# A graph-attention kernel on one core: another shape for the one-hot picks that replace part of the gathers

## The chip, the core and the metric

The kernel runs on one core of a Trainium2 chip. The metric is the device time of one execution in microseconds (us); three runs of the kernel before gave 4651.4 us as the median (4637.57 to 4661.18). The core's engines work side by side, each on its own queue of instructions in order: TensorE (PE, with its weight loads shown apart as PEld), VectorE (DVE), ScalarE (ACT), GpSimd (POOL) and SyncE (SP, which here only issues DMAs). They are tied together by semaphores.

## What is computed

Three layers of a graph transformer with 64 features, 6250 nodes and 206250 edges sorted by their target node, then a log-softmax, and a layer norm over the sum with the input. Cut to what matters here, one layer is

```python
q = x @ Wq + bq; k = x @ Wk + bk; v = x @ Wv + bv
e = edge_attr @ We
kj = k[src] + e
alpha = jnp.sum(q[dst] * kj, axis=-1) / jnp.sqrt(jnp.float32(D))
amax = jax.ops.segment_max(alpha, dst, num_segments=N)
p = jnp.exp(alpha - amax[dst])
denom = jax.ops.segment_sum(p, dst, num_segments=N)
w = p / denom[dst]
msg = (v[src] + e) * w[:, None]
agg = jax.ops.segment_sum(msg, dst, num_segments=N)
```

`x[src]` is the costly part: for each edge one row of 64 floats, from a place that the data decides, in every layer.

## The kernel before, in words

**Tiles.** Edges are cut into 403 chunks of 512 (`CH`), a chunk into four tiles (`T`) of 128. Four chunks (`LB`) make a batch, so a batch has 16 tiles and there are 101 batches. The program of all engines is written out in one order by Python generators (`tc.manual_schedule`): the main loop (L1660 to L1724) takes one batch as a "unit" u per round and interleaves sums of unit u-2 (`sums`, L1514), the transposed weights of u-1 (`weights`, L1506), the scores of u (`scores`, L1480), four turns of the next rows (`turn`, L1464), the ends of finished nodes (`finish`, L1309), and the picks for unit u+1.

**Rows by gather.** `gather` (L572) issues one indirect DMA from POOL for each tile of 128 edges (L578), which fetches 128 rows of x. `release` (L603) lets a chunk's gathers go when ACT has copied its indices to a `gate` tile (L609).

**Rows by pick.** In layer 0 the edges of each chunk are also sorted on the fly (`mark`, `Move`, `sorter`), so that tile t = 0 of each chunk has only source nodes of the first 18 blocks of 128 nodes (`RB`), and tile t = 3 only of the last 18. For some of those tiles no gather is issued; the rows are made on PE instead. `PICKS` says how many tiles of a batch: 3 in layer 0, 6 in layers 1 and 2, in the order of `spots` (t = 0 of chunks 0 to 3, then t = 3). `parts` holds the 36 blocks of x as a high and a low part. A source node in such a range has a block number 0 to 17, which is split into h, the group of `KB` = 4 blocks, and a place in the group; the key h*128 + (node mod 128) is compared with `rank` to give a one-hot.

The class `Picker` does this for two tiles (a pair) at a time:

- `aim` (L1169): two matmuls with the constant `coef` (L1182) spread the pair's keys over all partitions in PSUM (tag "m" in layers 1 and 2, "p" in layer 0); one DVE comparison (L1196) writes `NH` = 5 one-hots for both tiles, 128 x 1280 elements, to `hot`. Before the first pair of a batch, `which` (L1188) marks each edge's place in its group.
- `batch` (L1204): takes a pair, first aims the next one, then runs for each tile 5 groups x 2 parts = 10 matmuls (L1218; four groups of 256 columns and one of 128) into one half of a PSUM bank (tag "x", in layer 0 "s"); then DVE multiplies with `which` (L1229) and adds the four places in two steps (L1232, L1233), the last into the tile's place in the features.

`some` (L1652) advances the picks by a third of the batch's number of tiles at three places of a unit.

**Sorted order kept in DRAM.** `Move.drain` (L1010) writes a tile `to` with 32 rows for each chunk (five bits of the target's place, a row of ones, and the source node's numbers) to `toS` by one DMA of ACT's queue. Each later use loads it with one DMA of SP's (`decode`, L1604, three units ahead) into one of four `to` buffers. Both `aim` and `scores` read it; `scores` (L1484) multiplies it with `codeS`, 128 x 128. `Move.index` (L1033) computes the source indices in the new order and `kbs`, each edge's place in its group.

The picks' lines, and the order in which `aim` and the matmuls stand, are in the functions printed here:

Of the kernel before, what the change touches and what calls it, by code (L numbers as in the profile page):

```python
# [19 lines left out]
P = 128  # L20
D = 64
# [13 lines left out]
KB = 4  # L35
# [6 lines left out]
PICKS = ((3,), (6,), (6,))  # L42
LEAD = (4, 1, 1)


def slot(j):

    return j % 2 * (LB // 2) + j // 2
# [378 lines left out]
def main_path(  # L427
# [82 lines left out]
    tos = ctx.enter_context(tc.tile_pool(name="tos", bufs=4))  # L510
# [30 lines left out]
    toS = dram.tile([NT, P, CH], BF16, name="toS")  # L541
# [129 lines left out]
    def locate(k, m):  # L671

        half = CH // 2
        for i in range(2):
            at = slice(k * CH + i * half, k * CH + (i + 1) * half)
            room = picks.tile([P, NH, 2 * P], F32R, name="hot").rearrange("p h e -> p (h e)").bitcast(F32)
# [145 lines left out]
    codeS = const.tile([P, P], BF16, name="codeS")  # L822
    coef = const.tile([P, LB, P], BF16, name="coef")
    pickc = const.tile([P, 2, LB], BF16, name="pickc")
    kbs = const.tile([P, NT, 2, LB], BF16, name="kbs")
# [3 lines left out]
    def tools():  # L829
# [4 lines left out]
        room = picks.tile([P, 2, KB, D], F32, name="rows_of_b", bufs=1).rearrange("p s b d -> p (s b d)")  # L834
        two, wide = room[:, :LB], room[:, P : 2 * P]
        at = [ident[:, i::W] for i in range(ROW_K + 1)]
        nc.vector.scalar_tensor_tensor(two, at[ROW_H], float(P), at[ROW_P], ALU.mult, ALU.add)
        nc.vector.tensor_copy(coef, two.unsqueeze(2).to_broadcast([P, LB, P]))
        nc.vector.scalar_tensor_tensor(pickc[:, 0], at[ROW_B], float(P), at[ROW_P], ALU.mult, ALU.add)
        nc.vector.tensor_copy(pickc[:, 1], at[ROW_K])  # L840
        nc.vector.memset(wide, 0.0)
        for j in range(LB):
            rows = slice(slot(j) * W, (slot(j) + 1) * W)
            nc.vector.tensor_copy(wide[rows, j * W : j * W + BITS + 1], bit[rows, :])
        pc = ps("a")
        nc.tensor.transpose(pc[:, :P], wide, ident)
        nc.vector.tensor_scalar(codeS, pc[:, :P], FAR, None, ALU.mult)
# [6 lines left out]
    def mark(g):  # L854
# [56 lines left out]
        nc.vector.scalar_tensor_tensor(whole[1], lh[:, 1], -float(OFF), misc[:, ROW_B - 1], ALU.mult, ALU.add)  # L911
        yield
        nc.vector.tensor_scalar(whole[0], whole[1], KB.bit_length() - 1, None, ALU.logical_shift_right)
        nc.vector.tensor_copy(misc[:, ROW_H - 1], whole[0])
        nc.vector.tensor_scalar(whole[0], whole[1], KB - 1, None, ALU.bitwise_and)
        nc.vector.tensor_copy(misc[:, ROW_K - 1], whole[0])
# [24 lines left out]
    class Move:  # L941
# [68 lines left out]
        def drain(self):  # L1010
# [6 lines left out]
            nc.scalar.dma_start(toS[self.k], self.to)  # L1017
# [15 lines left out]
        def index(self):  # L1033

            k = self.k
            pi = ps("a")[:, : T * 2 * LB].rearrange("p (t v c) -> p t v c", t=T, v=2)
# [116 lines left out]
    class Picker:  # L1153


        def __init__(self, layer):
            self.layer = layer
            self.todo = []
            for k in range(len(batches)):
                those = spots(picked(layer, k))  # L1160
                for t in (0, T - 1):
                    cs = [c for c, i in those if i == t]
                    self.todo += [(k, t, cs[i : i + 2]) for i in range(0, len(cs), 2)]
            self.aimed = []
            self.which = {}
            self.side = 0
            self.keys = ps("m") if layer else None

        def aim(self):  # L1169

            if not self.todo or (self.layer, self.todo[0][0]) not in codes:
                return
            k, t, cs = self.todo.pop(0)
            n = len(cs)
            to = codes[self.layer, k]
            if self.layer:
                self.side = 1 - self.side
                pk = self.keys[:, self.side * 2 * P :][:, : n * P]
            else:
                pk = ps("p")[:, : n * P]  # L1180
            for s, c in enumerate(cs):
                nc.tensor.matmul(  # L1182
                    pk[:, s * P : (s + 1) * P], coef[:, c, :], to[:, t * P : (t + 1) * P], start=True, stop=True
                )
            if (self.layer, k) not in self.which:
# [9 lines left out]
            hot = picks.tile([P, NH, 2 * P], F32R, name="hot")[:, :, : n * P]  # L1195
            nc.vector.tensor_tensor(  # L1196
                hot,
                pk.unsqueeze(1).to_broadcast([P, NH, n * P]),
                rank.unsqueeze(2).to_broadcast([P, NH, n * P]),
                ALU.is_equal,  # L1200
            )
            self.aimed.append((k, t, cs, hot, self.which[self.layer, k]))

        def batch(self, k):  # L1204
# [3 lines left out]
            while self.aimed and self.aimed[0][0] == k:  # L1208
                _, t, cs, hot, which = self.aimed.pop(0)
                self.aim()  # L1210
                n = len(cs)
                px = ps("x" if self.layer else "s").rearrange("p (s b d) -> p s b d", s=2, b=KB)
                b0 = RB if t else 0
                for s in range(n):
                    for m, h in enumerate((0, *reversed(range(1, NH)))):
                        w = min(KB, RB - h * KB)
                        for i in range(2):
                            nc.tensor.matmul(  # L1218
                                px[:, s, :w].rearrange("p b d -> p (b d)"),
                                hot[:, h, s * P : (s + 1) * P],  # L1220
                                parts[:, i, b0 + h * KB : b0 + h * KB + w, :].rearrange("p b d -> p (b d)"),
                                start=(m == 0 and i == 0),
                                stop=(m == NH - 1 and i == 1),
                            )
                    if s + 1 < n:
                        yield
                at = (LB if t else 0) + cs[0]
                rows = picks.tile([P, 2, KB, D], F32, name="rows_of_b", bufs=1)[:, :n]
                nc.vector.tensor_tensor(  # L1229
                    rows, px[:, :n], which[:, at : at + n, :].unsqueeze(3).to_broadcast([P, n, KB, D]), ALU.mult  # L1230
                )
                nc.vector.tensor_tensor(rows[:, :, : KB // 2], rows[:, :, : KB // 2], rows[:, :, KB // 2 :], ALU.add)  # L1232
# [599 lines left out]
```

## Time and profile before

| what | value |
|---|---|
| median of three runs | 4651.4 us (4637.57 to 4661.18) |
| the profiled execution, its own time | 4656.6 us |
| its span, first to last instruction | 4654.9 us |
| mean granted TensorE clock | 0.966 |
| PE, PEld busy | 4216.7, 3111.6 us |
| DVE, ACT, POOL busy | 3829.2, 1995.7, 3337.9 us |
| gathers (POOL L578) | 3380 in all |
| pick matmuls (L1218) | 14560 |

The page divides the span into layer 0 (to about 1860 us, with the sorting), layer 1 (about 1980 to 3200 us) and layer 2 (about 3330 us to the end); between them PE's busy share falls for some 120 us. "Busy" is the union of an engine's instructions. In the group rows the numbers after the bar are busy us, mean ns of one, and the idle time of the engine just before, with what ended most of it; in the timeline the first column is the start in us from the span's start, the second the length of the merged run. A window view gives, for each engine, busy us and number of instructions.

### The profile page before, as it was taken

To read this page: it belongs to the slowest core of one execution; us is meant where nothing else is said; L and a number is where in the kernel's file an instruction comes from. 1 tells how busy PE (TensorE), PEld (TensorE's weight loads), DVE (VectorE), ACT (ScalarE), POOL (GpSimd) and SP (SyncE) were. 2 spreads that over 40 slices of the span, in tenths; PEclk is the share of its full clock that TensorE was granted. 3 is DMA by queue.
4 is the path that set the end of the run, shared out by engine and by line. 5 is a ranking of instruction groups with operands and counts; after the bars stand their busy time and mean duration, and the time that the engine had idled before them with its cause. 6 is when DMAs were issued, how large, how long until landed. Compare 5 with 4: busy or idle time off the path is not lost.

```text
span 4654.9 us, 117245 instructions
## 1 busy us (share of the span) xinstructions
PE 4216.7 (91%) x41145; PEld 3111.6 (67%) x41145; DVE 3829.2 (82%) x9064; ACT 1995.7 (43%) x5733; POOL 3337.9 (72%) x3390
## 2 busy tenths in 40 slices
PE   6889999999999999689999999999699999999996
PEld 3445555555555555367888888887478778878874
DVE  6778888898888888478888888888478888888885
ACT  2455555555555555333333333333234333334443
POOL 6777777777777766277777777777477777777774
PEclk9999999999999999799999999999799999999997
DMA  8787777777777777445555565555356655656553
GB/s 188 192 210 184 188 204 188 189 195 200 199 198 193 192 197 189 125 102 132 137 139 137 138 144 138 140 138 129 86 128 143 141 135 135 138 130 143 136 135 81
DMA packets 769749, 725.47 MB, mean 156 GB/s; under 512 B 403478, under 2 KB 544880, under 8 KB 769156
## 3 DMA queue, kind: packets, MB, share of 16 engines
q1 hardware_dynamic: 572564, 480.73, 43.5%
q0 software_dynamic: 108160, 110.97, 12.7%
q10 hardware_dynamic: 88432, 126.17, 7.7%
q8 instruction: 334, 5.47, 0.5%
q14 instruction: 259, 2.12, 0.2%
HBM read 557.62 MB, written 159.87 MB: 154 GB/s over the span
## 4 chain that ended last, share of the span: by engine, by line


## 5 line engine op out<-in xcount | busy, mean ns | idle before, releaser
L578 POOL DMA_INDIRECT feat<-x,gate x2004 | 1924.4, 960 | 613.9 <-issue 471.5
L578 POOL DMA_INDIRECT feat<-in_x,gate x1328 | 1365.8, 1028 | 526.2 <-issue 317.1
L1218 PE MATMUL ps_x<-parts,hot 128*128 128x256 f32 (+1 forms) x11880 | 1567.1, 288 | 0.0
L1218 PEld LDWEIGHTS ps_x<-parts,hot 128*128 128x128 f32 x11880 | 1457.1, 193 | 0.0
L1476 ACT COPY featT<-ps_a 64x256 f32<-64x256 f32 x2380 | 872.4, 367 | 1305.8 <-PE ps_a L1473 1265.2
L1196 DVE TENSOR_TENSOR hot<-ps_m,rank 128x1280 fp32r<-128x1280 f32 x594 | 879.9, 1481 | 33.1 <-PE ps_m L1182 32.9
L993 PE MATMUL ps_x<-hit,thirds 128*64 128x512 bf16 x4800 | 637.7, 393 | 5.5 <-DVE hit L983 5.1
L1473 PE MATMUL ps_a<-ident,feat 128*128 128x128 f32 x2380 | 488.0, 283 | 64.0 <-DMA feat<-x,gate 40.4
L983 DVE TENSOR_SCALAR hit<-ruler,pos 128x512 bf16<-128x512 f16 x1600 | 504.6, 363 | 1.7 <-PE ps_m L1002 1.5
L1473 PEld LDWEIGHTS ps_a<-ident,feat 128*128 128x128 f32 x2380 | 281.9, 140 | 333.4 <-issue 287.5
L1229 DVE TENSOR_TENSOR rows_of_b<-ps_x,which 128x512 f32<-128x512 f32 x594 | 406.4, 684 | 88.1 <-PE ps_x L1218 87.1
L1502 ACT ACTIVATE prob<-ps_s,part 128x512 f32<-128x512 f32 (+1 forms) x306 | 210.6, 688 | 625.6 <-DVE part L1500 500.0
L1218 PE MATMUL ps_s<-parts,hot 128*128 128x256 f32 (+1 forms) x2680 | 392.3, 294 | 30.9 <-ACT prob L1502 30.9
L993 PEld LDWEIGHTS <-thirds 128*64 128x64 bf16 x4800 | 233.2, 111 | 230.5 <-issue 83.6
L1218 PEld LDWEIGHTS ps_s<-parts,hot 128*128 128x128 f32 x2680 | 340.8, 195 | 60.7 <-ACT prob L1502 40.7
L1498 DVE TENSOR_REDUCE most<-ps_s 128x1 f32<-128x512 f32 (+1 forms) x306 | 211.2, 690 | 189.4 <-PE ps_s L1488 181.4
L1232 DVE TENSOR_TENSOR rows_of_b<-rows_of_b 128x256 f32<-128x256 f32 (+1 forms) x776 | 321.0, 414 | 26.6
L1522 PE MATMUL ps_g<-feat,probT 128*32 128x128 f32 x9672 | 338.2, 279 | 4.1 <-DVE y L1366 2.3
L1488 PE MATMUL ps_s<-featT,q 128*32 128x512 f32 x2418 | 336.3, 611 | 5.9 <-ACT featT L1469 5.2
L1522 PEld LDWEIGHTS ps_g<-feat,probT 128*32 128x32 f32 x9672 | 263.5, 111 | 52.6 <-issue 34.0
L1512 DVE COPY probT<-ps_p 128x512 f32<-128x512 f32 (+1 forms) x306 | 209.2, 684 | 99.0 <-PE ps_p L1510 97.3
L1182 PEld LDWEIGHTS <-coef 128*128 128x128 bf16 x1456 | 134.7, 99 | 190.5 <-issue 175.1
(226 smaller groups left out, 4392.6 us busy)
## 6 DMA issues: line engine op xcount, KB each, us to landing
feat<-eaP SPq DMA_DIRECT2D x296, 512.0 KB
featT<-eaS SPq DMA_DIRECT2D x296, 512.0 KB
raw<-in_ea SPq DMA_DIRECT2D x200, 256.0 KB
eaS<-eT ACTq DMA_DIRECT2D x200, 256.0 KB
eaP<-eN ACTq DMA_DIRECT2D x200, 256.0 KB
to<-toS SPq DMA_DIRECT2D x296, 128.0 KB
feat<-x,gate POOLq DMA_INDIRECT x2004
feat<-in_x,gate POOLq DMA_INDIRECT x1328
```

The costliest lines, as they stand in the source:

```text
L578: nc.gpsimd.indirect_dma_start(out=feat[:, c, t, 0], out_offset=None, in_=xts[layer][:, :], in_offset=bass.IndirectOffsetOnAxis(ap=index[: ...
L983: nc.vector.tensor_scalar(hit, ruler, self.pos[:, at : at + 1], None, ALU.is_equal)
L993: nc.tensor.matmul(self.px[i][j * D : (j + 1) * D, :], self.thirds[i][:, part, (j * T + t) * D : (j * T + t + 1) * D], self.hits[t, 2 * i ...
L1196: nc.vector.tensor_tensor(hot, pk.unsqueeze(1).to_broadcast([P, NH, n * P]), rank.unsqueeze(2).to_broadcast([P, NH, n * P]), ALU.is_equal,)
L1218: nc.tensor.matmul(px[:, s, :w].rearrange("p b d -> p (b d)"), hot[:, h, s * P : (s + 1) * P], parts[:, i, b0 + h * KB : b0 + h * KB + w, ...
L1229: nc.vector.tensor_tensor(rows, px[:, :n], which[:, at : at + n, :].unsqueeze(3).to_broadcast([P, n, KB, D]), ALU.mult)
L1232: nc.vector.tensor_tensor(rows[:, :, : KB // 2], rows[:, :, : KB // 2], rows[:, :, KB // 2 :], ALU.add)
L1473: nc.tensor.transpose(pt[:, t // 2 * P : (t // 2 + 1) * P], rows[:, t * D : (t + 2) * D], ident)
L1476: nc.scalar.copy(featT[:, :, h, :], pt[h * D : (h + 1) * D, : T // 2 * P].rearrange("d (i e) -> d i e", e=P))
L1488: nc.tensor.matmul(self.p_s[slot(j) * W : (slot(j) + 1) * W, :], self.q[:, j * STRIDE : j * STRIDE + W], self.featT[:, j, :], start=False, ...
L1498: nc.vector.tensor_reduce(top[:n], self.p_s[:n], AX.X, ALU.max)
L1522: nc.tensor.matmul(p_g[rows, :].rearrange("n (h d) -> n h d", h=2), self.probT[:, t, rows], batch[:, c + j, t], start=(t == 0), stop=(t == ...
```

## The change

Six blocks make a group instead of four (`KB` = 6), so 18 blocks need `NH` = 3 one-hots instead of 5, and a tile 6 matmuls of 384 columns each instead of 10. `PICKS` becomes 7, 6, 7 tiles in turn in layers 1 and 2 (6.67 on average); layer 0 stays at 3.

The keys are no longer spread by matmuls on each use. `Move.index` computes each batch's keys once (one matmul with `keyc`, one ACT copy) and stores them in DRAM as fp16 (`keyS`); `decode` loads a batch's keys to all partitions by one DMA, three units ahead, into one of three `keys` buffers. `aim` now takes all tiles of a batch with the same t at once (up to four), and makes its one-hots from `keys` in SBUF with `NH` DVE instructions, one for each group.

Each tile has a PSUM bank of its own: in layers 1 and 2 three in turn (two of tag "x" and "m"), in layer 0 "p" and "s" in turn. DVE multiplies for each tile, and one `tensor_reduce` for two tiles adds the six places.

`toS` keeps only the six rows of each chunk that `scores` needs; `drain` writes them with four DMAs. A unit loads its own 24 rows one unit ahead into one of two buffers, and `scores` always uses `codeT`. `mark` works out group and place with comparisons instead of shifts.

```diff
-KB = 4
+KB = 6
-PICKS = ((3,), (6,), (6,))
+PICKS = ((3,), (7, 6, 7), (7, 6, 7))
+MOST = max(n for p in PICKS for n in p)
...
-    tos = ctx.enter_context(tc.tile_pool(name="tos", bufs=4))
+    tos = ctx.enter_context(tc.tile_pool(name="tos", bufs=2))
...
-    toS = dram.tile([NT, P, CH], BF16, name="toS")
+    toS = dram.tile([NT, LB, BITS + 1, CH], BF16, name="toS")
+    keyS = dram.tile([NT, 2, LB, P], FP16, name="keyS")
...
-        nc.vector.tensor_scalar(whole[0], whole[1], KB.bit_length() - 1, None, ALU.logical_shift_right)
-        nc.vector.tensor_copy(misc[:, ROW_H - 1], whole[0])
-        nc.vector.tensor_scalar(whole[0], whole[1], KB - 1, None, ALU.bitwise_and)
-        nc.vector.tensor_copy(misc[:, ROW_K - 1], whole[0])
+        block, h = spare[:, 1], misc[:, ROW_H - 1]
+        nc.vector.scalar_tensor_tensor(block, lh[:, 1], -float(OFF), misc[:, ROW_B - 1], ALU.mult, ALU.add)
+        nc.vector.tensor_scalar(h, block, float(KB), None, ALU.is_ge)
+        for i in range(2, NH):
+            nc.vector.scalar_tensor_tensor(h, block, float(i * KB), h, ALU.is_ge, ALU.add)
+        nc.vector.scalar_tensor_tensor(misc[:, ROW_K - 1], h, -float(KB), block, ALU.mult, ALU.add)
...
-            nc.scalar.dma_start(toS[self.k], self.to)
+            for c in range(LB):
+                nc.scalar.dma_start(toS[self.k, c], self.to[c * W : c * W + BITS + 1])
...
+            pk = pa[:LB, 2 * P :].rearrange("c (t e) -> c t e", t=2)
+            nc.tensor.matmul(
+                pk, keyc, self.to.rearrange("r (t e) -> r t e", t=T)[:, :: T - 1], start=True, stop=True
+            )
+            key = small.tile([LB, 2, P], FP16, name="key", bufs=1)
+            nc.scalar.copy(key, pk)
+            nc.scalar.dma_start(keyS[k].rearrange("t c e -> c t e"), key)
...
-            for s, c in enumerate(cs):
-                nc.tensor.matmul(
-                    pk[:, s * P : (s + 1) * P], coef[:, c, :], to[:, t * P : (t + 1) * P], start=True, stop=True
-                )
...
-            hot = picks.tile([P, NH, 2 * P], F32R, name="hot")[:, :, : n * P]
-            nc.vector.tensor_tensor(
-                hot,
-                pk.unsqueeze(1).to_broadcast([P, NH, n * P]),
-                rank.unsqueeze(2).to_broadcast([P, NH, n * P]),
-                ALU.is_equal,
-            )
+            hot = picks.tile([P, NH, LB * P], F32R, name="hot", bufs=2)[:, :, : n * P]
+            for h in range(NH):
+                nc.vector.tensor_scalar(
+                    hot[:, h], keys[self.layer, k][:, first : first + n * P], rank[:, h : h + 1], None, ALU.is_equal
+                )
...
+                for s, c in enumerate(cs):
+                    px = ps(("xxm" if self.layer else "ps")[self.turn])[:, : KB * D].rearrange("p (b d) -> p b d", b=KB)
+                    self.turn = (self.turn + 1) % (3 if self.layer else 2)
+                    for h in range(NH):
...
+                    nc.vector.tensor_tensor(
+                        rows[:, s % 2], px, which[:, at].unsqueeze(2).to_broadcast([P, KB, D]), ALU.mult
+                    )
+                    if s % 2 or s + 1 == len(cs):
+                        n = s % 2 + 1
+                        nc.vector.tensor_reduce(
+                            loaded[self.layer, k][:, c - n + 1 : c + 1, t, 0],
+                            rows[:, :n].rearrange("p s b d -> p s d b"),
+                            AX.X,
+                            ALU.add,
+                        )
...
-            if self.placed:
-                self.to = codes[layer, self.k]
-                return
             self.to = tos.tile([P, CH], BF16, name="to")
+            here = toS[self.k] if self.placed else places[c : c + m]
+            nc.sync.dma_start(self.to[: m * (BITS + 1), :], here.rearrange("c b e -> (c b) e"))
...
-            codes[layer, k] = tos.tile([P, CH], BF16, name="to")
-            nc.sync.dma_start(codes[layer, k], toS[k])
+            keys[layer, k] = picks.tile([P, MOST * P], FP16, name="keys")
+            nc.sync.dma_start(
+                keys[layer, k][:, : n * P],
+                keyS[k].rearrange("t c e -> (t c e)")[: n * P].partition_broadcast(P),
+            )
```

76 lines of the change are left out of this document (21 added, 55 removed).

## The prediction

> **What bounds the kernel now.** I read the windows by stage first, then the groups of one stage, then the waits, then a timeline of one batch. One window inside layer 0 and one inside layer 1:
>
> ```profile
> core 0: us, PE busy (x) PEld busy (x) DVE busy (x) ACT busy (x) POOL busy (x), PEclk, DMA share, GB/s
> 500.00:1800.00 1300.00, 1217.86 (x12036) 744.35 (x12032) 1131.84 (x3401) 694.44 (x1771) 938.88 (x926) 0.99 0.77 194
> 2400.00:3200.00 800.00, 763.03 (x7718) 642.67 (x7710) 695.81 (x1277) 302.51 (x994) 607.19 (x633) 1.00 0.59 138
> ```
>
> By busy share PE bounds layer 1 (95%) and POOL (76%) has room. The groups of that window say otherwise:
>
> ```profile
> L578 POOL DMA_INDIRECT feat<-x,gate x633 | 607.8, 960 | 193.1 <-issue 145.5 <-DMA feat<-x,gate 25.6 <-ACT gate L609 9.4
> ...
> L1196 DVE TENSOR_TENSOR hot<-ps_m,rank 128x1280 fp32r<-128x1280 f32 x189 | 279.8, 1481 | 5.0 <-PE ps_m L1182 5.0
> ...
> L1229 DVE TENSOR_TENSOR rows_of_b<-ps_x,which 128x512 f32<-128x512 f32 x189 | 129.1, 683 | 16.9 <-PE ps_x L1218 16.9
> ...
> L1232 DVE TENSOR_TENSOR rows_of_b<-rows_of_b 128x256 f32<-128x256 f32 x190 | 81.3, 428 | 6.5
> ...
> L1233 DVE TENSOR_TENSOR feat<-rows_of_b 128x128 f32<-128x128 f32 x190 | 56.6, 298 | 6.8 <-DVE rows_of_b L1232 0.3
> ...
> L1498 DVE TENSOR_REDUCE most<-ps_s 128x1 f32<-128x512 f32 x63 | 43.5, 691 | 37.9 <-PE ps_s L1488 37.9
> ```
>
> 189 one-hot comparisons at 3 a batch are 63 batches in 800 us: 12.70 us a batch. POOL's row: 607.8 busy and 193.1 idle make 800.9, the whole window, and the idle time is 0.305 us ahead of each of 633 gathers. So gathers run back to back at 800/633 = 1.264 us, ten a batch (12.64 us): **POOL paces layers 1 and 2.** PE is close behind: 12.11 us busy a batch, and what it waits for is the one-hot:
>
> ```profile
> PE ps_m L1182 <- DVE hot L1196: 35.5, 32, 1.6
> ...
> PE ps_a L1473 <- DMA feat<-x,gate: 1.3, 3, 0.7
> ```
>
> DVE is busy 695.81/63 = 11.04 us. Three engines within 13% of each other: what comes after depends on all three, so I cost the change on each.
>
> **The change on POOL.** A mean of 6.67 picked tiles leaves 9.33 gathers: 9.33 x 1.264 = 11.80 us a batch, 0.90 less.
>
> **On PE.** One batch's picks in the timeline:
>
> ```profile
> 2507.47 0.68 DVE L1229 TENSOR_TENSOR rows_of_b<-ps_x,which 128x512 f32<-128x512 f32 x1
> 2507.61 0.27 PE L1182 MATMUL ps_m<-to,coef 128*128 128x128 bf16 x2 [0.88 <-DVE hot L1196]
> ...
> 2507.69 2.60 PE L1218 MATMUL ps_x<-parts,hot 128*128 128x256 f32 x20
> 2508.19 0.43 DVE L1232 TENSOR_TENSOR rows_of_b<-rows_of_b 128x256 f32<-128x256 f32 x1
> 2508.65 0.29 DVE L1233 TENSOR_TENSOR feat<-rows_of_b 128x128 f32<-128x128 f32 x1
> 2508.86 1.48 DVE L1196 TENSOR_TENSOR hot<-ps_m,rank 128x1280 fp32r<-128x1280 f32 x1
> ...
> 2510.24 0.25 PEld L1182 LDWEIGHTS <-coef 128*128 128x128 bf16 x2
> ...
> 2510.45 2.42 PEld L1218 LDWEIGHTS ps_x<-parts,hot 128*128 128x128 f32 x20
> ```
>
> A narrow view inside such a pair shows matmuls of 256 columns alone:
>
> ```profile
> 2508.47 0.76 PE L1218 MATMUL ps_x<-parts,hot 128*128 128x256 f32 x5
> ```
>
> Five starts, the last lasting 0.28: (0.76 - 0.28)/4 = 0.12 us from one to the next. A pair's 20 take (2.60 - 0.28)/19 x 20 = 2.44, so 1.22 a tile. A matmul of 384 columns isn't in the trace. If time goes by matmuls it costs 0.12 and a tile 6 x 0.12 = 0.72; if by columns 0.18 and a tile 1.08. I take the columns, the dearer: 6.67 x 1.08 = 7.20 against 6 x 1.22 = 7.32 (from below 4.80). The key matmuls go: their weight loads hold the path from 2510.24 to 2510.45, 0.21 us a pair, 0.63 a batch. The wait for the one-hot (35.5/63 = 0.56) should go too, since a group's one-hots are asked for a whole group of up to four tiles ahead instead of two. PE: 12.11 - 0.63 - 0.12 = 11.36 us. It no longer decides.
>
> **On DVE.** This is where the change pays. The prices of the new forms come from these rows (single lines' views, and groups over the whole span):
>
> ```profile
> L740 DVE TENSOR_SCALAR start<-start,low x4: 468/475/481, 18.6 to 141.4; 128x512 f32<-128x512 int32 x3, 19x512 f32<-19x512 int32 x1
> ...
> L1395 DVE TENSOR_SCALAR y<-y,lse x49: 242/247/444, 3568.7 to 4646.1; 128x64 f32<-128x64 f32 x49
> ...
> L1229 DVE TENSOR_TENSOR rows_of_b<-ps_s,which 128x256 f32<-128x256 f32 x96 | 39.3, 410 | 3.0 <-PE ps_s L1218 3.0
> ...
> L1389 DVE TENSOR_REDUCE lse<-ex 128x4 f32<-128x256 f32 x11 | 4.5, 410 | 0.0
> ...
> L983 DVE TENSOR_SCALAR hit<-ruler,pos 128x512 bf16<-128x512 f16 x1600 | 504.6, 363 | 1.7 <-PE ps_m L1002 1.5
> ```
>
> - One-hot, SBUF to SBUF, a scalar of each partition, four bytes out: L740 is nearest, 0.475 us at 512 elements; with L1395 (0.247 at 64) the slope gives 0.41 at 384 and 0.345 at 256. I add 0.03 for outliers like L1395's 444. Seven tiles: 3 x (0.51 + 0.44) = 2.85; six: 3 x (0.51 + 0.375) = 2.66; mean 2.79. From below 3 x 2 x 0.36 = 2.2 (the hit's price), from above the present comparison's 1.16 ns an element: 6.67 x 384 x 1.16 = 2.97.
> - Multiply from PSUM: between 0.410 (256) and 0.683 (512), 0.547 at 384; x 6.67 = 3.65.
> - `tensor_reduce` over two tiles, 768 elements read at a step of 64: 0.410 (256, L1389) and 0.691 (512) give 0.97; 0.55 for one tile. Seven: 3 x 0.97 + 0.55 = 3.46; six 2.91; mean 3.28. All rows of this operation read neighbours, so the stride's price is the unknown: below, 0.97; above, see the rivals.
>
> Added 9.72. Removed 3 x (1.481 + 0.683 + 0.428 + 0.298) = 8.67. Summed like this DVE goes to 11.04 + 1.05 = 12.1. But lengths overlap where nothing is awaited: the comparison at 2508.86 starts 0.08 us before L1233 ends (2508.94), while L1232 starts 0.04 after L1229 ends. Before, some two such joints a pair (0.4 a batch); after, about twelve (hot to hot, hot to multiply, multiply to multiply, reduce to the next) at 0.07: 0.8. So 11.04 + 1.05 - 0.4 = 11.7 busy, with small gaps of some 0.3 **about 12.0 us**; without any overlap gained, 12.5.
>
> Bank waits: a tile needs the bank of the tile three before, so PE can run three tiles (3.2 us) ahead of DVE; DVE's work between, the score maximum and a group's one-hots, is 0.69 + 1.4. I count nothing for it.
>
> **Together,** layers 1 and 2 go from 12.70 to the slowest of 11.80, 11.36 and 12.0, and I add 0.15 for engines that are so level: 12.15. Saved 0.55 x 99 batches x 2 = 109 us.
>
> The Trainium skill has a rule against this: "SBUF — State Buffer", "Who interferes with whom": a VectorE op in a two-port mode, which `tensor_scalar` in SBUF can enter, locks GpSimd out for the whole instruction. The one-hots move from a PSUM read to just that. This case's rows on it:
>
> ```profile
> L578 POOL DMA_INDIRECT feat<-x,gate x2004 | 1924.4, 960 | 613.9 <-issue 471.5 <-DMA feat<-x,gate 66.5 <-ACT gate L609 30.9
> ...
> L578 POOL DMA_INDIRECT feat<-in_x,gate x1328 | 1365.8, 1028 | 526.2 <-issue 317.1 <-ACT gate L609 122.9 <-DMA feat<-in_x,gate 14.6
> ```
>
> A gather takes 1028 in layer 0, where 1600 hits hold DVE 504.6 of 1860 us (27%), and 960 without them. If all 68 ns come from the hits, one-hots at 2.79/12.15 = 23% add 58: POOL 9.33 x 1.32 = 12.3, rival 2 below. If no gather went on during a one-hot, POOL would take 11.80 + 2.79 = 14.6, rival 5; by the rule taken whole that would be so, but then the hits' 27% would have stretched layer 0's gathers by more than 7%.
>
> **Layer 0.** The same groups in the window 500 to 1800:
>
> ```profile
> L578 POOL DMA_INDIRECT feat<-in_x,gate x926 | 940.0, 1015 | 361.4 <-issue 220.1 <-ACT gate L609 84.3 <-ACT mm L1329 10.1
> ...
> L1196 DVE TENSOR_TENSOR hot<-ps_p,rank 128x1280 fp32r<-128x1280 f32 x71 | 105.0, 1479 | 0.0
> ...
> L1196 DVE TENSOR_TENSOR hot<-ps_p,rank 128x640 fp32r<-128x640 f32 x71 | 57.6, 811 | 8.8 <-PE ps_p L1182 8.8
> ```
>
> 71 batches, 1300/71 = 18.31 us each; POOL's 926/71 = 13 gathers at 1.015 + 0.305 make 17.2, PE 17.15, DVE 15.9, ACT 9.8. PE: three tiles save 3 x 0.14 = 0.42, key matmuls in two groups about 0.35; the one new key matmul in each move I put at 0.15, below a pair's 0.21: -0.6. DVE: 1.479 + 0.811 become 3 x 0.44 (-0.97); multiplies, 3 x 0.547, and reduces, 0.97 + 0.55, against a pair's 1.41 and a single's 0.9: +0.85, so even. ACT: one copy of a 256-column PSUM tile (0.4, as DVE's) and four more DMA issues at
>
> ```profile
> L1017 ACTq DMA_DIRECT2D toS<-to x100: 326/326/377, 71.3 to 1915.1; - x100
> L1608 SPq DMA_DIRECT2D to<-toS x296: 319/590/1487, 109.7 to 4554.4; - x148
> ```
>
> 0.33: +1.7 us on a queue 53% busy. Behind `drain`'s issues stand the copy of the sums and the exponent; both have until the next unit. On SP one load more a batch, 0.59 us. In layer 0 it waits for `keyS` to land, which `index` stores two steps of the sorter after `drain`; behind it stand the next round's feature, q and `eaS` loads. Since `moved` lets it out only three steps after `index`, I count no wait. Transfers change little: 256 KB of `toS` traffic become some 150. PE's 0.6 meets POOL's 17.2 and ACT; I count half, 0.3 x 96 = 28 us.
>
> **Sum:** the profiled run's 4656.6 - 109 - 28 = 4520. The median of the three runs lies 5 below that run, so the forecast is **4515 us**.
>
> **Rivals.**
>
> 1. *DVE paces at its plain sum,* 12.5 (no overlap gained): 0.2 x 198 + 28 = 68 saved, 4583. For it: it needs no luck. Against it, the 0.08 that the timeline shows at such joints.
> 2. *Gathers lengthen* as bounded above, POOL 12.3: 0.4 x 198 + 28 = 107, 4544. For it 1028 against 960; against, layer 0 has other DVE work that the hits are lumped with.
> 3. *Slower: the strided reduce.* If an element at a step of 64 costs twice, 768 take about 1.75 us and 384 0.95; a batch's reduces go from 3.28 to 5.9, DVE to 14.6, above 12.70: +1.9 x 198 = 376 in layers 1 and 2 (in layer 0 DVE's room takes the 1.2): about 5010. It decides from 12.7 on, where a pair's reduce costs 1.18. Against it, two copies that read at a step of 64 too:
>
> ```profile
> L971 DVE COPY stamp<-misc x100: 209/220/333, 56.6 to 1882.5; 128x80 bf16<-128x80 bf16 x100
> L972 DVE COPY stamp<-misc x100: 195/204/249, 56.7 to 1882.6; 128x64 bf16<-128x64 bf16 x100
> ```
>
> 16 elements more cost 16 ns, about one a ns. The Trainium skill ("SBUF — State Buffer", "Door 1: The DMA port swizzle") states that a read that leaves a 16-byte line each time pays a penalty; by it this rival would hold, and these rows, bf16 and a copy, speak against it.
>
> 4. *No change:* PE's wait for the one-hot returns as a wait for PSUM banks, since three tiles in a row stand at two of the three places; a batch stays at 12.6 to 12.7 and ACT's issues eat layer 0's gain: 4640.
>
> 5. *Gathers stop during one-hots,* 14.6 a batch: +1.9 x 198 - 28, about 5000.
>
> **Chances.** Forecast 0.50, rival 1 0.22, rival 2 0.07, rival 3 0.11, rival 4 0.07, rival 5 0.03. The floor is POOL's 11.80 with all of layer 0's 0.6: 0.90 x 198 + 58 = 236, 4415. The range 4415 to 4645 takes in rivals 1, 2 and 4; alone, the forecast has 4450 to 4570. A measurement can tell 0.5%, 23 us, from no change: below 4628 faster. Faster: 0.50 + 0.22 + 0.07 less 0.03 for their tails, 0.76; same 0.09, rival 4 and those tails in part; slower 0.15, rivals 3 and 5 and the rest.
>
> **What would show it.** In layers 1 and 2: 28 gathers for three batches still back to back, and about 12.1 us a batch; L1182 gone, no PE wait for `hot`; matmuls of 384 columns 0.18 us apart or less; one-hots near 0.48 us, multiplies 0.55, reduces 0.97 and 0.55. I am wrong if a reduce takes over 1.2 us, if POOL's gathers pass 1.03 us, or if POOL idles over 0.31 ahead of each, which would say that another engine paces.

## The result and the profile after

The changed kernel takes **5169.68 us** (median of 4 runs, 5166.95 to 5171.33) against 4650.34 for the kernel before in the same series: ratio 1.1117, 95% interval [1.1088, 1.1146]. It is 11% slower. The forecast was 4515, the range ended at 4645, and the sign was wrong. In some of the series below every kernel, the one before too, takes 6210 to 6515 us (in one such profile no engine is busy over 79% of a window in layer 1 and the granted clock is 0.88; why is open), so ratios are always to the kernel before in the same series.

The two profiled executions are 515 us apart (5171.33 and 4656.6). Where these went shows in the distance from one score maximum (one DVE instruction a batch) to the next, and in the time of each layer's last one, both from the traces:

| kernel | layer 0, batches 20 to 90 | layer 1, batches 8 to 93 | layer 2, batches 8 to 93 | last score maximum of layers 0, 1, 2 |
|---|---|---|---|---|
| before | 18.39 us a batch | 12.65 | 12.65 | 1960.0, 3302.2, 4629.8 |
| after | 21.78 | 13.54 | 13.51 | 2314.6, 3736.3, 5144.9 |

Layer 0 loses 355 us, layers 1 and 2 lose 79 and 81. So there are two separate losses, and the larger stands in the layer where I expected 28 us of gain.

**Layers 1 and 2.** The windows of the changed kernel, to be held against the two of before (the same columns: PE, PEld, DVE, ACT, POOL busy, granted clock, DMA share, GB/s):

```profile
500.00:1800.00 1300.00, 1117.97 (x9333) 670.11 (x9332) 989.25 (x2866) 614.54 (x1560) 769.43 (x780) 0.90 0.61 159
2400.00:3200.00 800.00, 719.22 (x5680) 581.21 (x5678) 768.80 (x1418) 279.35 (x934) 546.35 (x567) 0.98 0.55 137
```

In the second row DVE is busy 768.80 of 800 us, 96%, where it had 87%: **DVE paces layers 1 and 2 now.** The groups of the window 2700 to 3500, different shapes apart:

```profile
L580 POOL DMA_INDIRECT feat<-x,gate x551 | 533.2, 968 | 267.8 <-ACT gate L611 118.6 <-issue 118.6 <-PE ps_g L1507 9.4
...
L1222 DVE TENSOR_REDUCE feat<-rows_of_b 128x128 f32<-128x768 f32 x177 | 268.3, 1516 | 6.1
L1217 DVE TENSOR_TENSOR rows_of_b<-ps_x,which 128x384 f32<-128x384 f32 x262 | 139.4, 549 | 8.7 <-PE ps_x L1207 1.8
...
L1188 DVE TENSOR_SCALAR hot<-keys,rank 128x512 fp32r<-128x512 f16 x177 | 76.7, 488 | 0.0
...
L1188 DVE TENSOR_SCALAR hot<-keys,rank 128x384 fp32r<-128x384 f16 x117 | 42.4, 417 | 0.0
L1483 DVE TENSOR_REDUCE most<-ps_s 128x1 f32<-128x512 f32 x59 | 40.0, 678 | 0.0
L1222 DVE TENSOR_REDUCE feat<-rows_of_b 128x64 f32<-128x384 f32 x39 | 32.3, 829 | 1.4
L1188 DVE TENSOR_SCALAR hot<-keys,rank 128x256 fp32r<-128x256 f16 x60 | 19.4, 377 | 0.0
```

59 batches. The one-hots (488, 417, 377 ns) and the multiply (549) came in where the prediction had them. The reduce over two tiles takes **1.516 us, not 0.97**, the one over a single tile 0.829, not 0.55. POOL idles 0.486 us ahead of a gather (267.8/551), and ACT's gate ends as much of that as "issue" (118.6 us each), which is time in which POOL waited for nothing that the profile shows; before, three quarters were issue (145.5 of 193.1): it no longer paces. PE's tile costs what the columns said. From its timeline:

```profile
2718.42 2.35 PE L1207 MATMUL ps_x<-parts,hot 128*128 128x384 f32 x12
2720.61 1.21 PE L1207 MATMUL ps_m<-parts,hot 128*128 128x384 f32 x6
```

Twelve matmuls from 2718.42 to the start of the next at 2720.61 are 0.183 us each; 0.18 was forecast.

**Layer 0.** In the first window every engine is busy for less time than before and none is full, and PE's granted clock is 0.90 instead of 0.99. The waits of the window 700 to 1700 (46 batches; us in total, times, longest):

```profile
POOL feat L580 <- ACT gate L611: 252.6, 111, 6.8
...
PE ps_a L1039 <- ACT key L1036: 94.6, 44, 6.0
...
ACT part L1515 <- DMA toS<-to: 33.6, 9, 4.5
```

The second line is new: PE waits 2.06 us a batch for the copy of the keys. The timeline of one such place:

```profile
1199.23 1.28 ACT L1290 ACT_TABLE_LOAD   x1
...
1200.37 0.38 PE L1032 MATMUL ps_a<-to,keyc 128*4 128x256 bf16 x1
...
1201.20 0.30 ACT L1290 ACTIVATE dev<-mv,eps 128x4 f32<-128x4 f32 x1 [0.69 <-DVE mv L1288]
1201.41 0.60 ACT L955 CAST thirds<-raw 128x512 bf16<-128x512 f32 x1
...
1202.03 0.36 ACT L1036 CAST key<-ps_a 4x256 f16<-4x256 f32 x1
...
1202.44 0.25 PE L1039 MATMUL ps_a<-pickc,to 128*128 128x8 bf16 x4 [1.70 <-ACT key L1036]
```

The key matmul is short (0.38). But the index matmuls behind it write the same PSUM bank, and the copy of the keys out of that bank stands between the two in the written order. So PE, which runs its queue in order, waits until ACT has worked off what is queued ahead of that copy: here a table load, the layer norm's deviation and a cast. By this reading everything behind the index matmuls on PE is late by that, the turned rows for the scores among it, and with them ACT's gates and the gathers; the first run below tests it.

### The profile page after: what moved, and what is told of

Read it like the earlier page. It is cut to its first block, busy times and chain, and to the rows that moved or that the text cites. A ratio compares the mean times of both kernels' runs of the same rounds, so it can differ in the third digit from the quotient of the medians.

```text
span 5169.6 us, 106393 instructions
## 1 busy us (share of the span) xinstructions
PE 4378.1 (85%) x34756; PEld 3095.8 (60%) x34756; DVE 4284.0 (83%) x9900; ACT 2038.6 (39%) x5833; POOL 3190.3 (62%) x3258
## 4 chain that ended last, share of the span: by engine, by line
## 5 line engine op out<-in xcount | busy, mean ns | idle before, releaser
L580 POOL DMA_INDIRECT feat<-x,gate x1872 | 1812.7, 968 | 874.0 <-issue 415.6
L1222 DVE TENSOR_REDUCE feat<-rows_of_b 128x128 f32<-128x768 f32 (+1 forms) x908 | 1217.9, 1341 | 31.8 <-DVE rows_of_b L1217 0.4
L1207 PE MATMUL ps_x<-parts,hot 128*128 128x384 f32 x5280 | 1123.6, 355 | 135.7 <-DVE rows_of_b L1217 129.9
L1207 PEld LDWEIGHTS ps_x<-parts,hot 128*128 128x128 f32 x5280 | 940.1, 196 | 198.2 <-DVE rows_of_b L1217 187.0
L1207 PE MATMUL ps_m<-parts,hot 128*128 128x384 f32 x2640 | 576.6, 354 | 69.2 <-DVE rows_of_b L1217 67.6
L1461 PEld LDWEIGHTS ps_a<-ident,feat 128*128 128x128 f32 x2380 | 333.1, 146 | 419.5 <-issue 275.5
L1188 DVE TENSOR_SCALAR hot<-keys,rank 128x512 fp32r<-128x512 f16 (+2 forms) x1476 | 567.7, 439 | 3.7 <-issue 3.6
L1207 PEld LDWEIGHTS ps_m<-parts,hot 128*128 128x128 f32 x2640 | 470.5, 196 | 98.2 <-DVE rows_of_b L1217 94.6
L1217 DVE TENSOR_TENSOR rows_of_b<-ps_x,which 128x384 f32<-128x384 f32 x880 | 468.6, 550 | 54.1 <-PE ps_x L1207 30.5
L1217 DVE TENSOR_TENSOR rows_of_b<-ps_m,which 128x384 f32<-128x384 f32 x440 | 241.8, 550 | 16.4 <-PE ps_m L1207 4.7
```

Source lines behind the costliest of these rows:

```text
L580: nc.gpsimd.indirect_dma_start(out=feat[:, c, t, 0], out_offset=None, in_=xts[layer][:, :], in_offset=bass.IndirectOffsetOnAxis(ap=index[: ...
L1188: nc.vector.tensor_scalar(hot[:, h], keys[self.layer, k][:, first : first + n * P], rank[:, h : h + 1], None, ALU.is_equal)
L1207: nc.tensor.matmul(px[:, :w].rearrange("p b d -> p (b d)"), hot[:, h, s * P : (s + 1) * P], parts[:, i, b0 + h * KB : b0 + h * KB + w, :]. ...
L1217: nc.vector.tensor_tensor(rows[:, s % 2], px, which[:, at].unsqueeze(2).to_broadcast([P, KB, D]), ALU.mult)
L1222: nc.vector.tensor_reduce(loaded[self.layer, k][:, c - n + 1 : c + 1, t, 0], rows[:, :n].rearrange("p s b d -> p s d b"), AX.X, ALU.add,)
L1461: nc.tensor.transpose(pt[:, t // 2 * P : (t // 2 + 1) * P], rows[:, t * D : (t + 2) * D], ident)
```

## The experiments

The kernel before took 4657.03 us beside the first four runs.

**The two losses, each undone alone.** First the copy of the keys and its store are moved behind the index matmuls and the two DVE instructions that read them:

```diff
-            key = small.tile([LB, 2, P], FP16, name="key", bufs=1)
-            nc.scalar.copy(key, pk)
-            nc.scalar.dma_start(keyS[k].rearrange("t c e -> c t e"), key)
             for t in range(T):
...
             nc.vector.tensor_copy(kbs[:, k], pi[:, 0 :: T - 1, 1])
+            key = small.tile([LB, 2, P], FP16, name="key", bufs=1)
+            nc.scalar.copy(key, pk)
+            nc.scalar.dma_start(keyS[k].rearrange("t c e -> c t e"), key)
```

> The key copy (ACT) and its DMA stand behind the index matmuls instead of between them and the key matmul; nothing else is moved. Theory: layer 0 lost its 350 us because PE, in order, waits for ACT to copy the keys out of a bank before it may write the index products into the same bank (2.06 us a batch in the window 700 to 1700), and because the matmuls after each such stall run at a lower granted clock (0.89 against 0.98). Then this row of PE waits vanishes, a layer-0 batch falls from 21.8 to 18.4 us or less, and the time to 4840 (4970 if only the wait itself comes back). Rival: layer 0 lost it to ACT's longer queue of DMA issues and to picks that now share banks with scores and weights; then the time stays over 5100. Both: layers 1 and 2 stay at 13.4 to 13.7 us a batch.

Measured: 4911.74 us (4902.14 to 4931.94), ratio 1.0558 [1.0525, 1.059], 258 us less, between the two times that the theory named. Layer 0 goes from 21.78 to 19.19 us a batch, layers 1 and 2 stay (13.51, 13.52). PE's wait for the copy is gone from the list, and the granted clock of the window 500 to 1500 is 0.96:

```profile
500.00:1500.00 1000.00, 921.61 (x8188) 539.04 (x8186) 862.91 (x2528) 530.80 (x1362) 703.60 (x685) 0.96 0.70 180
```

2.59 us a batch were won where the wait itself was 2.06, so the place of three lines costs a half of the whole loss, but not all of layer 0's: 0.8 us a batch is left.

Second, the reduce is replaced by three additions of neighbouring elements:

```diff
-                        nc.vector.tensor_reduce(
-                            loaded[self.layer, k][:, c - n + 1 : c + 1, t, 0],
-                            rows[:, :n].rearrange("p s b d -> p s d b"),
-                            AX.X,
-                            ALU.add,
-                        )
+                        half = rows[:, :n, : KB // 2]
+                        nc.vector.tensor_tensor(half, half, rows[:, :n, KB // 2 :], ALU.add)
+                        nc.vector.tensor_tensor(rows[:, :n, 0], rows[:, :n, 0], rows[:, :n, 1], ALU.add)
+                        nc.vector.tensor_tensor(
+                            loaded[self.layer, k][:, c - n + 1 : c + 1, t, 0], rows[:, :n, 0], rows[:, :n, 2], ALU.add
+                        )
```

> The tensor_reduce is replaced by three adds of neighbouring halves (3 blocks + 3 blocks, then two of one block); layer 0's copy stays where the change put it. Theory: DVE paces layers 1 and 2 (96% busy) through the reduce, 1.516 us for two tiles. Adds cost 0.56 + 0.30 + 0.30 and two joints, about 1.2: 0.3 x 3 + 0.1 less a batch, 12.7 us, 5000 in all. Rival: gathers or PSUM banks pace them; then DVE gets idle time and a batch stays at 13.4 to 13.7, 5150.

Measured: 5054.83 us (5052.24 to 5055.56), ratio 1.0851 [1.0833, 1.0869], 115 us less, where 170 were expected. Layer 0 stays at 21.78, layers 1 and 2 go to 12.85. The groups of the window 2700 to 3400:

```profile
L580 POOL DMA_INDIRECT feat<-x,gate x511 | 512.2, 1002 | 189.5 <-issue 116.1 <-ACT gate L611 48.0 <-DVE rows_of_b L1217 6.7
...
L1223 DVE TENSOR_TENSOR rows_of_b<-rows_of_b 128x384 f32<-128x384 f32 x163 | 91.2, 559 | 5.6
...
L1225 DVE TENSOR_TENSOR feat<-rows_of_b 128x128 f32<-128x128 f32 x163 | 48.0, 295 | 12.2 <-DMA feat<-x,gate 2.6 <-DVE rows_of_b L1224 2.1 <-DMA q<-qq 0.4
L1224 DVE TENSOR_TENSOR rows_of_b<-rows_of_b 128x128 f32<-128x128 f32 x163 | 47.8, 293 | 5.7
```

A pair's three additions take 559 + 293 + 295 = 1.147 us against the reduce's 1.516. DVE is still the fullest: 651.85 of that window's 700 us, 93%.

Both edits together:

> Both edits. If the two causes are independent the gains add: 5170 - 330 - 170 = 4670, near the kernel before. Rival: PE's stall and DVE's load hide each other, the sum falls short by 50 us or more.

Measured: 4790.49 us (4783.29 to 4794.74), ratio 1.0281 [1.0262, 1.0299]: 379 us less, of 258 + 115. The gains add, so the two causes are separate; each was sized too large in the expectation, and 133 us of the loss are left.

**Is it the stride?** With the late copy, the multiply writes its products so that the six places of a feature are neighbours, and the reduce reads neighbours; its element count is the same:

```diff
-                        rows[:, s % 2], px, which[:, at].unsqueeze(2).to_broadcast([P, KB, D]), ALU.mult
+                        rows[:, s % 2].rearrange("p b d -> p (b d)").rearrange("p (d b) -> p b d", b=KB),
+                        px,
+                        which[:, at].unsqueeze(2).to_broadcast([P, KB, D]),
+                        ALU.mult,
...
-                            rows[:, :n].rearrange("p s b d -> p s d b"),
+                            rows[:, :n].rearrange("p s b d -> p s (b d)").rearrange("p s (d b) -> p s d b", b=KB),
```

> As e1, and the multiply writes its products with the six places side by side (writes at a step of 6 elements), so that the reduce reads neighbours; same 768 elements, same 128 results. If the step of 64 is what costs, the reduce falls from 1.52 to 0.97 us, DVE to 11.8 us a batch, gathers pace again at 12.0, and the time is 4530. If each of the 128 short sums costs a few cycles, the reduce stays at 1.5 and the time at e1's 4840. If writing at a step of 6 costs, the multiply goes from 0.55 to over 0.9 and eats it.

Measured: 4899.78 us (4893.32 to 4910.6), ratio 1.0521 [1.0499, 1.0544], layers 1 and 2 at 13.47 and 13.46: almost nothing against the late copy alone. But the groups tell the cause:

```profile
L1217 DVE TENSOR_TENSOR rows_of_b<-ps_x,which 128x384 f32<-128x384 f32 x230 | 188.8, 856 | 7.3 <-PE ps_x L1207 0.5 <-DVE feat L1225 0.5 <-PE ps_m L1207 0.5
...
L1225 DVE TENSOR_REDUCE feat<-rows_of_b 128x128 f32<-128x768 f32 x155 | 147.7, 953 | 5.3
...
L1225 DVE TENSOR_REDUCE feat<-rows_of_b 128x64 f32<-128x384 f32 x34 | 18.8, 553 | 1.2
```

Reading neighbours, the reduce takes 0.953 and 0.553 us, the prediction's 0.97 and 0.55 to 2%. So the reduce's extra 0.56 us is the price of the step. And the step can't be had for nothing on the other side: the multiply that writes at a step of six elements goes from 0.549 to 0.856.

**What is left.** Three edits on top of the late copy and the three additions. Six tiles in every batch of layers 1 and 2 (`PICKS = ((3,), (6,), (6,))`):

> The changed kernel with the late key copy and the three adds (it took 4790 us), but six picked tiles in every batch of layers 1 and 2 instead of 6.67. Theory: with the adds DVE still sets the pace of these layers (12.9 us a batch, DVE 93% busy), and 0.67 tile less frees it by 0.67 x (hots 0.4 + multiply 0.55 + adds 0.58) = 1.0 us, to 11.9; but ten gathers at 1.27 to 1.29 us make 12.7 to 12.9, so POOL takes over and nothing is won: 4760 to 4800 us. This would say that the choice of 6.67 isn't what costs. Rival: the seven-tile batches themselves are what is slow (PE's and DVE's queues run dry between the groups of four and three), then six tiles bring 12.4 or less, under 4700 us.

One store of the bucket rows instead of four, with a load that takes its 24 rows out of it:

```diff
-            for c in range(LB):
-                nc.scalar.dma_start(toS[self.k, c], self.to[c * W : c * W + BITS + 1])
+            nc.scalar.dma_start(toS[self.k], self.to)
...
+                nc.sync.dma_start(
+                    self.to[: m * (BITS + 1), :], toS[self.k].rearrange("(c w) e -> c w e", w=W)[:m, : BITS + 1]
+                )
```

> The late key copy and the three adds, and the bucket rows stored by one DMA of 128 partitions from ACT's queue as before, instead of four of six rows; the loads take their 24 rows out of it. Theory: in layer 0 ACT is held by the issues, since the copy of the attention sums stands behind them and now waits 127.8 us in 53 batches (2.4 us each) against 31.2 in 55 before; three issues less at 0.33 us take 1.0 us off it and layer 0 goes from 19.26 to about 18.85 us a batch: 40 us less, 4750 us. Rival: what is left of layer 0's loss is in PE's order (key matmul and banks), ACT's issues are beside it, and the time stays at 4780 to 4800.

And the copy of the transposed probabilities on ACT in layers 1 and 2:

```diff
-            nc.vector.tensor_copy(self.probT[:, :, :n], p_t[:, :, :n])
+            if self.layer:
+                nc.scalar.copy(self.probT[:, :, :n], p_t[:, :, :n])
+            else:
+                nc.vector.tensor_copy(self.probT[:, :, :n], p_t[:, :, :n])
```

> The late key copy and the three adds, and in layers 1 and 2 ACT (36% busy there) copies the transposed probabilities out of PSUM instead of DVE: 0.68 us a batch off DVE. Theory: DVE paces layers 1 and 2 even with the adds, so they go from 12.88 to about 12.3 us a batch, where POOL's 9.33 gathers at 1.29 (12.05) and PE (11.95 busy) come near: 115 us less, 4675 us. Rival: PE's chain of scores, exponent and sums paces, and ACT's in-order queue makes the copy later than DVE did: 4790 us or more.

These three gave 6504.28, 6301.28 and 6298.75 us, beside 6410.84 for the kernel before (ratios 1.0137, 0.9835, 0.9832). The expectations name times of 4675 to 4800, so none of them can be judged by these. The last two were run again; six tiles come again further down, with all four edits:

> The same kernel as the one with one store of 128 partitions, run again beside its neighbours, since the chip of the last call ran the kernel before at 6411 us and its ratios can't be set beside those of the earlier runs. If this chip runs the kernel before at about 4655 us: theory (ACT's issues hold layer 0) 4750 us, ratio 1.020; rival (they are beside the path) 4790, ratio 1.028 as without the edit.

> The same kernel as the one in which ACT copies the transposed probabilities in layers 1 and 2, run again. Theory (DVE paces these layers): 12.3 us a batch, 4675 us, ratio 1.004. Rival (PE's chain paces, ACT's queue makes the copy later): 12.9 a batch, ratio 1.028 or more.

> All four edits together: late key copy, three adds, one store, probabilities copied by ACT in layers 1 and 2. If the causes are separate the gains add: 4790 - 40 - 115 = 4635 us, ratio 0.996 to the kernel before. If layers 1 and 2 then meet POOL's 12.05 and no less, at best 4600 us; if PE's order sets both, 4700 or more.

The kernel before took 4656.12 us beside these. One store: 4719.55 us (4711.43 to 4725.28), ratio 1.0134 [1.0112, 1.0155], 71 us less than without it, where 40 were expected; layer 0 goes from 19.26 to 18.53 us a batch. The row of the copy of the sums in the window 500 to 1500, first with four stores, then with one (the last two numbers ahead of the releasers: mean ns, and us of idle time before it):

```profile
L1515 ACT COPY part<-ps_g 128x128 f32<-128x128 f32 x53 | 14.1, 265 | 127.8 <-DMA toS<-to 36.3 <-DMA eaS<-eT 29.2 <-PE ps_a L1461 20.6
```

```profile
L1518 ACT COPY part<-ps_g 128x128 f32<-128x128 f32 x54 | 14.3, 265 | 28.0 <-PE ps_s L1474 22.9 <-PE ps_a L1464 3.1 <-PE ps_s L1476 1.6
```

The time that ACT stands ahead of this copy falls from 2.41 to 0.52 us a batch, and the DMA issues are gone from its releasers. Three issues at 0.31 us make 0.9 of these 1.9 us; what made the rest is not shown. PE needs the same PSUM tag for the ends of nodes: with four stores it waits for this copy, "PE ps_g L1269 <- ACT part L1515", 17.3 us in those 53 batches and in a second place, L1355, 11.4, with one store 0.4 us in all. So ACT's issues reach PE, and these waits are 0.54 of the 0.73 us won a batch.

Probabilities on ACT: 4707.61 us (4702.05 to 4712.86), ratio 1.0104 [1.0086, 1.0123], 83 us less, where 115 were expected; 12.42 and 12.31 us a batch in layers 1 and 2, close to the theory's 12.3. All four edits: **4627.1 us** (4626.6 to 4633.32), ratio 0.9935 [0.9918, 0.9952], expected 4635. It is faster than both kernels, than the one before by 0.65% only. The window 2500 to 3200 and its gathers:

```profile
2500.00:3200.00 700.00, 664.34 (x5404) 538.35 (x5404) 643.67 (x1740) 302.90 (x944) 528.38 (x529) 1.00 0.61 147
```

```profile
L580 POOL DMA_INDIRECT feat<-x,gate x529 | 528.7, 999 | 171.9 <-issue 125.7 <-ACT gate L611 19.5 <-ACT part L1521 5.9
```

Of POOL's idle time 125.7 of 171.9 us are issue, about the share of before the change, and it idles 0.325 us ahead of a gather: the gathers run back to back again, but at 700/529 = 1.323 us each instead of 1.264. PE, with 95% of the window, and DVE, with 92%, are close behind.

**Is the share of picked tiles worth its gathers?** Six tiles in the version with all four edits, and as a check on "POOL paces" the kernel before with the probabilities on ACT. The pair was run three times beside a kernel before that took 6290, 6270 and 6415 us, the third time with all four edits and 6.67 tiles beside it; a fourth series has the six tiles alone:

> All four edits, but six picked tiles in every batch of layers 1 and 2. In the kernel with all four, gathers of layer 2 run back to back again, 1.302 us each (900 us for 691), so POOL paces it. Theory: ten gathers instead of 9.33 then cost 0.67 x 1.30 = 0.87 us a batch, less what shorter gathers give back (with fewer adds beside them, 1.27 to 1.30): 12.7 to 13.0 us a batch against 12.3 to 12.46, that is 4690 to 4760 us, ratio 1.007 to 1.022. It would show that the share of picked tiles is worth what its gathers cost once DVE is out of the way. Rival: DVE or PE still paces and six tiles are no slower: 4600 to 4640 us.

> The kernel before, in which ACT instead of DVE copies the transposed probabilities in layers 1 and 2, 0.68 us a batch off DVE. Theory: POOL's ten gathers pace these layers there, so nothing changes: within 0.4%, 4640 to 4675 us. Rival: DVE (11 us busy) or PE's wait for the one-hot has a share in 12.65, and the copy's 0.68 shows up: 4560 to 4620 us; then a part of what the version with all four edits wins isn't the change's.

> The version with all four edits and six picked tiles, run again, since the chip of the last call ran the kernel before at 6290 us. Theory: POOL paces, ten gathers instead of 9.33 cost 0.87 us a batch less what shorter gathers give back: 12.7 to 13.0 us a batch against 12.3 to 12.46, 4690 to 4760 us, ratio 1.007 to 1.022. Rival: DVE or PE still paces and six tiles are no slower: 4600 to 4640 us, ratio 0.99 to 0.997.

> The kernel before with the transposed probabilities copied by ACT in layers 1 and 2, run again. Theory: POOL's ten gathers pace these layers, nothing changes: within 0.4%, 4640 to 4675 us. Rival: DVE or PE's wait for the one-hot has a share in 12.65 us, and it gets faster by 0.8% or more: 4560 to 4620 us.

> The version with all four edits once more, as the neighbour of the next two. On a chip that runs the kernel before at 4655 us: 4627 us, ratio 0.9935 as before. On one that runs it at 6270 us: the four edits lower the same busy times there, ratio 0.97 to 0.985.

> All four edits with six picked tiles. Theory (POOL paces once DVE is relieved): 12.7 to 13.0 us a batch in layers 1 and 2, 4690 to 4760 us, 1.3 to 2.8% above its neighbour with 6.67. Rival (DVE or PE still paces): at or under its neighbour.

> The kernel before with the transposed probabilities copied by ACT in layers 1 and 2. Theory (POOL's ten gathers pace these layers): within 0.4% of the kernel before. Rival (DVE has a share): faster by 0.8% or more.

> All four edits with six picked tiles, for a chip that runs the kernel before at about 4655 us. Theory (POOL paces once DVE is relieved, 1.27 to 1.30 us a gather): 12.7 to 13.0 us a batch in layers 1 and 2, 4690 to 4760 us, ratio 1.007 to 1.022. Rival (DVE or PE still paces): no slower than with 6.67, ratio 0.9935 or less.

In the first three series the six tiles had ratios of 1.0072, 1.0076 and 0.9999, the last beside 0.9738 [0.9676, 0.98] for all four edits with 6.67 tiles (6412.0 against 6258.45 us, 2.5% more, where 1.3 to 2.8 were expected); the kernel before with the probabilities on ACT had 0.9965, 0.9983 and 0.9956 [0.9928, 0.9984]. In the fourth the kernel before took 4652.85 us, and six tiles take 4730.07 us (4722.66 to 4745.36), ratio 1.0176 [1.015, 1.0203], 12.96 and 12.99 us a batch, inside the theory's 12.7 to 13.0. Its gathers in the window 2500 to 3200:

```profile
L580 POOL DMA_INDIRECT feat<-x,gate x542 | 535.4, 988 | 165.2 <-issue 122.8 <-DMA feat<-x,gate 19.8 <-ACT gate L611 7.3
```

Back to back at 700/542 = 1.292 us, ten a batch: 12.92. So the 0.67 tile is worth 1.0176 - 0.9935 = 2.4% once DVE is out of the way. The same run says something about the new shape by itself: with six tiles, as many as the kernel before picks, it is 1.8% slower than that kernel although DVE is busy for less of the window (571.76 of 700 us against 608.80), and ten gathers of 988 ns instead of 960 make 0.28 of the 0.3 us that a batch of layers 1 and 2 takes longer. The gain over the kernel before comes with the 0.67 tile; 6.67 tiles in the old shape weren't tried. Whether DVE has any share in the 12.65 us of the kernel before stays open: the probabilities on ACT were tried there only in series in which it took over 6260 us, and gave 0.2 to 0.4%. So a part of the 0.65% may be that edit's and not the change's.

## Why the prediction was wrong

**The reduce (a term mis-sized).** The step "768 elements read at a step of 64 ... give 0.97; 0.55 for one tile" took the price of neighbours. Measured: 1.516 and 0.829. A batch has 3 pairs and 39/59 of a single: 3 x 1.516 + 0.66 x 0.829 = 5.1 us of reduces instead of 3.28. With these 1.8 us more the predicted 12.0 becomes 13.8; measured are 13.5. So the reduce covers the whole gap in layers 1 and 2, and the rest of DVE's sum was some 0.3 us too high. This is rival 3, with its own threshold: it was to decide from 1.18 us on. (Its "about 5010" is 4651 + 376 - 28 = 4999 by its own terms.) The rows that spoke against it, two copies of bf16 at about one element a ns, didn't carry over to a reduce of four-byte elements; which of the two differences matters wasn't tried. The Trainium skill's "SBUF — State Buffer", "Door 1: The DMA port swizzle", says that a read that moves on to another 16-byte line each time pays a penalty. The trace agrees with that (1516 against 953 ns for the same 768 elements). I gave this rival a chance of 0.11.

**Layer 0 (a wait not seen).** "The one new key matmul in each move I put at 0.15" was right for the matmul and wrong for the step: it costed instructions and didn't ask what stands behind the copy of their result. "I count no wait" was meant for SP's loads; the wait came on PE, for ACT, through the shared bank. Undoing it gave 258 us. ACT's "+1.7 us on a queue 53% busy", said to have time until the next unit, was the second: three stores less gave 71 us, since the copy of the sums stands behind them and PE waits for its bank. With both undone layer 0 stands at 18.53 us a batch against 18.39 before, so the 0.3 of gain forecast for it wasn't there either. No rival had layer 0 losing anything.

**POOL.** That POOL paced before is the right reading, but not by the sum given for it: busy and idle time of POOL's only large row fill the window whatever paces. What tells is that three quarters of the idle time were issue, in which POOL waited for nothing that shows. 1.264 us a gather held in form, not in size. In the changed kernel POOL idles 0.486 us ahead of each, beyond the 0.31 that the prediction named as its own refutation. Where gathers pace again, 9.33 of them cost 1.323, 12.3 us a batch: the price of rival 2. But not for its reason: beside the one-hots alone, in the changed kernel, a gather takes 968 ns against 960 before; it goes to about 1000 only with the three additions (965 to 970 in the three kernels without them, 995 to 1007 in the five with them and 6.67 tiles, windows 2500 to 3200 and 3800 to 4400). Why they lengthen it is not shown. The other rule that the prediction took from the Trainium skill ("SBUF — State Buffer", "Who interferes with whom") is that GpSimd is locked out during a two-port VectorE instruction. Beside the one-hots no more than those 8 ns show, and whether they run in such a mode no run shows; rival 5 is out.

**DVE's other terms, PE and the banks.** One-hots were 0.488, 0.417 and 0.377 us for 0.51, 0.44 and 0.375 in the sum; the multiply (0.549 for 0.547) and PE's matmul (0.183 for 0.18) were right to 2%. PE's sum was too low: 664.34/700 of 12.38 us, a batch's time in that window, is 11.75 a batch in the version with all edits, 11.36 was forecast; which of its terms fell short isn't known. The bank waits, for which it counted nothing, are there: PE waits for `rows_of_b` 54.4 us in the window 2400 to 3200 of the changed kernel, 0.92 us a batch, and 25.5 us in the window 2500 to 3200 with all four edits, 0.45 a batch. They shrink as DVE's load does, which fits DVE being late as their cause but doesn't show it.

**The forecast's idea** that fewer gathers buy time was right in direction: with all four edits 6.67 tiles beat six by 2.4%. Layers 1 and 2 then take 12.46 and 12.30 us a batch, where 12.15 was forecast.

## What to carry to other kernels

Price a strided read or write by a row with the same step, type and operation, and where there is none, let the range hold twice the price of neighbours: here the step cost 59% on the read and 56% on the write. When a result that an in-order engine copies shares a PSUM bank with the next matmuls, put the copy behind them, and look at what is queued ahead of it on that engine; the cost is that queue, not the copy. An engine that is half busy is no cover by itself: ask who waits for the instruction that stands behind the added issues.

## What was not expected of the hardware

- An issue of a store of six partitions held ACT's queue hardly less than one of 128 partitions, so four held it for 1.23 us by their median against 0.33. Issue times (smallest, median, largest in ns) of the four in the changed kernel, then of the one before:

```profile
L1010 ACTq DMA_DIRECT2D toS<-to x400: 263/308/1188, 68.6 to 2268.9; - x134
```

```profile
L1017 ACTq DMA_DIRECT2D toS<-to x100: 326/326/377, 71.3 to 1915.1; - x100
```

- PE's granted clock in layer 0 fell with its waits: 0.99 before and 0.89 after in the window 500 to 1500, 0.96 with the late copy, 0.98 with one store and the additions too. The late copy won 2.59 us a batch where the wait was 2.06; no run parts the clock from the wait.
